# Keys, values and transposed context of the first block, made between the scores of its first unit

## The chip, the cores and the metric

The kernel runs on one core of a Trainium2 chip. Its time is the device time of one execution in microseconds (us). The figure for the kernel before is the median of three runs. Everything else about it comes from one further execution under the hardware profiler.

## The reference, cut to what matters

Four cross-attention layers follow each other on one sequence x of 2048 rows by 256; all read one context of 1601 rows by 512. Layers 0, 2 and 3 are of this form, with 16 heads of 64 (inner width 1024):

```python
q = hidden_states @ Wq                      # 256 -> 1024
k = encoder_hidden_states @ Wk              # 512 -> 1024
v = encoder_hidden_states @ Wv
logits = jnp.einsum('bhqd,bhkd->bhqk', q, k) * HEAD_DIM ** (-0.5)
col_bias = col_bias.at[:, token_indices_A].set((-SUPPRESS * suppress_A_in)[:, None])
col_bias = col_bias.at[:, token_indices_B].set((-SUPPRESS * suppress_B_in)[:, None])
probs = jax.nn.softmax(logits + col_bias, axis=-1)
out = jnp.einsum('bhqk,bhkd->bhqd', probs, v)
out = out @ Wo + bo + residual
```

Two of the 1601 keys for each of A and B (which ones is an input) get a bias that depends on the query row through a mask of 2048 values. Layer 1 has an RMS norm ahead of it, 16 query heads of 16 and 4 key heads, and no bias. All is in float32.

## The kernel before, in words

**Tiles and units.** Keys are cut into 13 chunks (`TCH`, NT = 13): twelve of 128 rows and one of 65. Queries are cut into NB = 4 parts of 512 rows (`QB`). A masked layer has 8 blocks of two heads. A block has four units, one for each query part. A unit runs over the 13 chunks; a step is one chunk of one unit, so a block is 52 steps, and the main loop (L1093) takes steps in pairs. The unit's scores of step s are taken by `masked_scores` (L669): two heads' matmuls into one PSUM pair tile, a copy into a tile of `probs` by ScalarE (L687) and a running maximum by VectorE (L690, L692). When all 13 are done, `maxima` (L728) transposes the maximum on TensorE (L735), reduces it (L736), and sends it through DRAM on to all partitions (L643, L646). The exponentials of the same unit run NT+5 = 18 steps behind its scores: `maxima_spread` (L751) copies the spread maximum into PSUM, `subtract` (L756) is VectorE, `masked_exp` (L761) is ScalarE, and GpSimd adds up the sums (L764, L766). The product with the values (`values`, L801) runs 20 steps behind. So in the steady state TensorE has, for each chunk, scores of one unit and values of an earlier one.

**Pieces.** Work that is not part of a step is kept as pieces with a cost: a unit's queries (L451), denominators (L822), projection (L850), and the keys and values of the next block. `start_block(i)` (L965) loads block i+1's weights and makes its pieces: seven of keys (two chunks of context each, L427) and seven of values (L381). Each takes a context slice that `context_slice` (L245) reads back from DRAM, three slices ahead, into a tile of `work` (`ct`, three buffers). Keys go into `pieces.fill` and values into `pieces.later`, which is released when the last unit of the block before has its values done (L1045), inside the current block; in block 0 that does not happen. A pair of steps takes its due pieces, and, when it scores and exponentiates (`together`, L1130), about one piece of `fill`. At a block's first step `pieces.flush()` (L1032) runs whatever is left.

**The opening.** Before the loop, in this order: the loads of x on ScalarE's DMA queue (L135 to L139); token numbers on SyncE's (`token_numbers`, L147); `key_order` (L164), VectorE arithmetic that puts the biased keys at the end of the context, so that the bias falls into the last chunk: it finds, for each of 13 columns of positions and each of 65 tail positions, the row it comes from (`src`, L223 to L236, 78 columns by 12 tokens); then `first_x` (L574), which transposes x on TensorE, and the first unit's queries. Then L897 to L902 make all keys and values of block 0: `first_context_slice` (L253) gathers the rows of the context by indirect DMA on GpSimd's queue (L260), transposes them on TensorE (L266), copies them out of PSUM, half by ScalarE and half by VectorE, and stores them to DRAM as `ctxT` (L274). Only then does the loop begin. At the third pair of steps `token_rows` (L298) loads the two masks (L301, L302), works them into bias rows (three bfloat16 parts, transposes at L325), and makes `tail_keys` for each masked layer (L332 to L344).

**What sets the order.** L1145 to L1151 tie TensorE, ScalarE and VectorE to the order in which the code writes their instructions. SyncE and GpSimd, with their DMAs, are ordered by the framework's scheduler. Keys, values, queries and bias transposes share one PSUM tile (`pm`, one buffer); score tiles have two buffers (`s`), and a third tile of the same size (`b`) holds the spread maximum. `probs` has 22 buffers. Matmuls of float32 show as two records each.

Of the kernel before, what the change touches and what calls it, by code (L numbers as in the profile page):

```python
# [10 lines left out]
FP = mybir.dt.float32  # L11
# [23 lines left out]
def tile_cross_attention_stack(ctx: ExitStack, tc: tile.TileContext, t: dict, out: bass.AP):  # L35
# [99 lines left out]
    x_rows = [probs.tile([P, QT, C], FP, name="p") for _ in range(NB)]  # L135
    for b in range(NB):
        nc.scalar.dma_start(
            out=x_rows[b], in_=x[0, ts(b, QB), :].rearrange("(n p) c -> p n c", p=P)
        )  # L139
# [7 lines left out]
    def token_numbers():  # L147

        idx = const.tile([P, NTOK], I32, name="tok_idx")
        for l, name in enumerate(masked_names):  # L150
            for s, which in ((0, "A"), (2, "B")):
                nc.sync.dma_start(
                    out=idx[:, 4 * l + s : 4 * l + s + 2],
                    in_=t[name + "token_indices_" + which]
                    .rearrange("(o s) -> o s", o=1).to_broadcast((P, 2)),
                )
# [7 lines left out]
    def key_order(tok):  # L164
# [50 lines left out]
        wide = [P, N, NTOK]  # L215

        def tokens_of(v):
            return v.rearrange("p (o j) -> p o j", o=1).to_broadcast(wide)

        def at_positions(v):  # L220
            return v.rearrange("p (n o) -> p n o", o=1).to_broadcast(wide)

        test = probs.tile(wide, FP, name="p")  # L223
        src = const.tile([P, N], FP, name="src")
        spec = probs.tile([P, N], FP, name="p")
        place = probs.tile([P, N], FP, name="p")
        nc.vector.tensor_tensor(test, at_positions(pos), tokens_of(where), ALU.is_ge)
        nc.vector.tensor_reduce(src, test, AX.X, ALU.add)
        nc.vector.tensor_tensor(src, src, pos, ALU.add)

        nc.vector.tensor_scalar(place, pos, count, float(T), ALU.add, ALU.subtract)
        nc.vector.scalar_tensor_tensor(src, place, 0.0, src, ALU.is_lt, ALU.mult)
        nc.vector.tensor_tensor(test, at_positions(place), tokens_of(rank), ALU.is_equal)
        nc.vector.tensor_tensor(test, test, tokens_of(mine), ALU.mult)
        nc.vector.tensor_reduce(spec, test, AX.X, ALU.add)
        nc.vector.tensor_tensor(src, src, spec, ALU.add)  # L236
        rows = const.tile([P, NT], I32, name="src_rows")
        nc.vector.tensor_copy(rows, src[:, :NT])
        return rows, src[:, NT:]
# [13 lines left out]
    def first_context_slice(i):  # L253

        tiles = [probs.tile([P, 2, 512], FP, name="p") for _ in range(NCT // 2)]
        a0, n0 = TBK[i]
        for c in range(4 * i, min(4 * i + 4, NT)):
            a, n = TCH[c]
            rows = probs.tile([P, CT], FP, name="p")
            nc.gpsimd.indirect_dma_start(  # L260
                out=rows[:n, :], out_offset=None, in_=cond[0],
                in_offset=bass.IndirectOffsetOnAxis(ap=src_rows[:n, c : c + 1], axis=0),
            )
            pt = psum.pair((NCT, P))
            for k in range(NCT):
                nc.tensor.transpose(pt[:, k, :n], rows[:n, ts(k, P)], ident[:n, :n])  # L266
            for k, ct in zip(range(0, NCT, 2), tiles):
                to = ct[:, :, a - a0 : a - a0 + n]
                if k:
                    nc.vector.tensor_copy(to, pt[:, k : k + 2, :n])  # L270
                else:
                    nc.scalar.copy(to, pt[:, k : k + 2, :n])
        for k, ct in zip(range(0, NCT, 2), tiles):
            nc.sync.dma_start(out=ctxT_dram[:, k : k + 2, a0 : a0 + n0], in_=ct[:, :, :n0])  # L274
        return lambda c, k: tiles[k // 2][
            :, k % 2, TCH[c][0] - a0 : TCH[c][0] - a0 + width(c)
        ]
# [20 lines left out]
    def token_rows():  # L298
# [4 lines left out]
        nc.vector.tensor_scalar(masks, masks, -1.0, 1.0, ALU.mult, ALU.add)  # L303
        nc.vector.tensor_scalar(masks, masks, -SUPPRESS, None, ALU.mult)
        bias_cols = probs.tile([P, QT, P], FP, name="p")
        nc.gpsimd.memset(bias_cols, 0.0)
        parts = probs.tile([P, 6, NQ], FP, name="p")
        for m in range(2):
            three_parts(masks[:, m, :], [NQ], lambda i: parts[:, 3 * m + i, :])

        row_of = small.tile([P, 2], FP, name="row_of", bufs=1)
        for j, (r0, r1) in enumerate(((RA, RB), (RB, RE))):
            for h in HALVES:
                nc.vector.tensor_reduce(
                    row_of[h : h + 64, j : j + 1], ident[h : h + 64, h + r0 : h + r1], AX.X, ALU.add
                )
        for b in range(NB):
            for h in HALVES:
                nc.vector.tensor_copy(
                    bias_cols[:, :, h + RA : h + RE],  # L320
                    parts[:, :, b * QT : (b + 1) * QT].rearrange("p r q -> p q r"),
                )
# [4 lines left out]
        for l in range(NL):  # L327


            marks = probs.tile([P, 2, NTAIL], FP, name="p")  # L330
            for to, j in ((0, 0), (1, 2)):
                nc.vector.tensor_scalar(  # L332
                    marks[:, to, :], src_tail, tok[:, 4 * l + j : 4 * l + j + 1], None,
                    ALU.is_equal,
                )
                nc.vector.scalar_tensor_tensor(
                    marks[:, to, :], src_tail, tok[:, 4 * l + j + 1 : 4 * l + j + 2],
                    marks[:, to, :], ALU.is_equal, ALU.max,
                )
            only = probs.tile([P, NTAIL], FP, name="p")  # L340
            nc.vector.tensor_tensor(only, marks[:, 0, :], marks[:, 1, :], ALU.is_gt)

            nc.vector.tensor_scalar(tail_keys[l], only, row_of[:, 0:1], None, ALU.mult)
            nc.vector.scalar_tensor_tensor(  # L344
                tail_keys[l], marks[:, 1, :], row_of[:, 1:2], tail_keys[l], ALU.mult, ALU.add
            )

    bo_of = []
    with nc.allow_non_contiguous_dma(reason="columns of 256 values"):
        for name in masked_names:  # L350
            bo_of.append(const.tile([P, NC], FP, name="bo_" + name))
            nc.gpsimd.dma_start(out=bo_of[-1], in_=t[name + "bo"].rearrange("(k p) -> p k", p=P))
    normw = const.tile([P, NC], FP, name="normw")
    with nc.allow_non_contiguous_dma(reason="one column of 256 values"):
        nc.gpsimd.dma_start(out=normw, in_=t["L1_xattn_norm_w"].rearrange("(k p) -> p k", p=P))

    QUARTERS = (0, 32, 64, 96)  # L360
    den_rows = const.tile([P, 4], FP, name="den_rows")
    one_row = const.tile([P, 1], FP, name="one_row")
    sel = const.tile([64, 4, 4, 32], FP, name="sel")
    nc.gpsimd.memset(sel, 0.0)
# [820 lines left out]
```

## Time and profile before

| What | us |
|---|---|
| median of three runs | 4948.83 (4944.98 to 4951.98) |
| the profiled execution, its own time | 4952.0 |
| its span, first to last instruction | 4950.3 |
| TensorE busy, of the span | 4747.6 (96%) |
| VectorE busy | 3752.7 (76%) |
| first scores of the first unit | 69.42 |
| first scores of block 1 | 243.63 |

The busy shares are of the whole span; the change is in its first 250 us, so windows and the timeline of that stretch say more. Lines of the timeline give the start, the duration, the engine, the line of code and the operation, output first, and in brackets how long the engine was idle and what ended that. Lines of windows give, for each stretch, TensorE's busy time, its weight loads, VectorE, ScalarE and GpSimd, each with a count of instructions, and then the granted TensorE clock, the DMA engines' busy share and GB/s. "PE" is TensorE, "DVE" VectorE, "ACT" ScalarE, "POOL" GpSimd, and "SP" SyncE.

### The profile page before, as it was taken

What the parts mean: (1) busy time and instruction counts of PE and PEld (TensorE: products, weight loads), DVE (VectorE), ACT (ScalarE), POOL (GpSimd) and SP (SyncE); (2) the same over time, 40 slices, a digit from 0 to 9 for tenths busy, and PEclk for the clock granted to TensorE, in tenths of its full rate; (3) what the DMA queues carried; (4) which work ended last, traced back from release to release, by engine and by line L of the source; (5) the groups of instructions that cost most, each with busy time, mean ns of one, the idle gap of its engine ahead of it and who ended that gap; (6) DMA issues with size and microseconds to landing.
All of it is one profiled execution on the core that took longest, in us unless ns stands there. A gap on an engine that the chain in (4) does not pass through costs nothing.

```text
span 4950.3 us, 64060 instructions
## 1 busy us (share of the span) xinstructions
PE 4747.6 (96%) x24004; PEld 2061.6 (42%) x24004; DVE 3752.7 (76%) x3782; ACT 3218.1 (65%) x4000; POOL 2988.8 (60%) x1429
## 2 busy tenths in 40 slices
PE   6899999999999999999999999999999999999996
PEld 4344444444444444444344444444444444444432
DVE  3788888888765666554378888888888888888886
ACT  2677777777634555444467777777777777777774
POOL 1677777777720000000177777777777777777787
PEclk9999999999989999999799999999999999999998
DMA  4222222222201000012133232232222322223211
GB/s 140 65 79 81 80 83 82 81 85 75 71 26 37 19 19 19 26 29 59 29 91 87 77 86 79 82 88 77 78 85 84 84 82 78 79 83 86 78 29 34
DMA packets 352534, 337.88 MB, mean 68 GB/s; under 512 B 120697, under 2 KB 306297, under 8 KB 352224
## 3 DMA queue, kind: packets, MB, share of 16 engines
q1 hardware_dynamic: 348960, 328.41, 23.5%
q8 instruction: 189, 3.10, 0.3%
q0 software_dynamic: 1152, 3.28, 0.2%
q10 hardware_dynamic: 2112, 2.10, 0.1%
q14 instruction: 121, 0.99, 0.1%
HBM read 318.89 MB, written 14.82 MB: 67 GB/s over the span
## 4 chain that ended last, share of the span: by engine, by line
PE 85%; DVE 10%; issue 1%; POOL 1%; ACT 1%; DMA 1%; SPq 0%; POOLq 0%; DVEq 0%; ACTq 0%
PE po L801 27%; PE s L675 19%; PE t L706 8%; PE pm L381 6%; PE pm L427 6%; PE s L850 4%; PE pm L451 4%; PE t L771 3%; DVE rden L826 2%; DVE ntop L736 2%; PE s L822 2%; DVE xs L862 2%; PE s L735 2%; DVE top L692 1%; DVE p L756 1%
## 5 line engine op out<-in xcount | busy, mean ns | idle before, releaser
L766 POOL TENSOR_TENSOR sums<-sums,p 128x1024 f32<-128x1024 f32 (+1 forms) x1152 | 2726.6, 2367 | 754.0 <-ACT p L761 582.2
L687 ACT COPY p<-s 128x1024 f32<-128x1024 f32 (+1 forms) x1248 | 1235.0, 1014 | 680.5 <-PE s L675 590.5
L801 PE MATMUL po<-p,v 128*64 128x512 f32 (+3 forms) x8320 | 1512.2, 531 | 10.4 <-ACT p L761 6.7
L756 DVE TENSOR_TENSOR p<-p,b 128x1024 f32<-128x1024 f32 (+1 forms) x1248 | 1460.9, 1209 | 56.1 <-ACT b L751 54.9
L692 DVE TENSOR_TENSOR top<-s,top 128x1024 f32<-128x1024 f32 (+1 forms) x1056 | 1290.6, 1222 | 233.0 <-ACT p L687 169.6
L675 PE MATMUL s<-q,kT 64*128 64x512 f32 (+1 forms) x4992 | 1348.5, 634 | 91.8 <-DVE ntop L736 23.7
L761 ACT ACTIVATE p<-p 128x1024 f32<-128x1024 f32 (+1 forms) x1248 | 1254.9, 1057 | 51.7 <-DVE p L756 50.3
L801 PEld LDWEIGHTS po<-p,v 128*64 128x64 f32 (+3 forms) x8320 | 368.0, 126 | 1106.3 <-issue 865.3
L675 PEld LDWEIGHTS s<-q,kT 64*128 64x128 f32 (+1 forms) x4992 | 390.6, 182 | 741.8 <-issue 210.2
L783 ACT ACTIVATE p<-t 128x512 f32<-128x512 f32 (+1 forms) x760 | 412.3, 594 | 414.8 <-PE t L706 377.5
L719 DVE TENSOR_REDUCE row_top<-t 128x1 f32<-128x512 f32 x700 | 451.0, 686 | 260.4 <-PE t L706 257.7
L842 POOL TENSOR_TENSOR oT<-oT,by 128x512 f32<-128x512 f32 x112 | 142.9, 1275 | 764.5 <-DMA by<-cols 423.6
L706 PE MATMUL t<-kT,q 32*128 32x512 f32 (+1 forms) x1880 | 562.6, 642 | 0.0
L771 PE MATMUL t<-q,kT 32*128 32x512 f32 (+1 forms) x1520 | 493.7, 662 | 0.0
L706 PEld LDWEIGHTS t<-kT,q 32*128 32x128 f32 x1880 | 294.9, 316 | 168.8 <-issue 84.3
L381 PEld LDWEIGHTS pm<-wv,ct 128*128 128x128 f32 (+1 forms) x2496 | 290.2, 188 | 130.7 <-issue 71.2
L381 PE MATMUL pm<-wv,ct 128*128 128x128 f32 (+2 forms) x2496 | 322.5, 282 | 6.9 <-ACT v L385 3.2
L427 PE MATMUL pm<-ct,wk 128*128 128x256 f32 (+1 forms) x1288 | 301.1, 377 | 0.6 <-DMA wk<-in_L_xattn_Wk_dram 0.6
L736 DVE TENSOR_REDUCE ntop<-s 128x8 f32<-128x1024 f32 x96 | 117.5, 1224 | 229.0 <-PE s L735 229.0
L427 PEld LDWEIGHTS pm<-ct,wk 128*128 128x128 f32 x1288 | 221.0, 190 | 150.0 <-issue 93.6
L764 POOL COPY sums<-p 128x1024 f32<-128x1024 f32 x96 | 99.5, 1036 | 203.2 <-ACT p L761 203.2
L850 PE MATMUL s<-oT,wo 128*128 128x512 f32 x392 | 199.6, 632 | 17.5 <-POOL oT L842 13.6
(155 smaller groups left out, 2356.2 us busy)
## 6 DMA issues: line engine op xcount, KB each, us to landing
ct<-ctxT SPq DMA_DIRECT2D x288, 512.0 KB
xT<-xT SPq DMA_DIRECT2D x100, 512.0 KB
spread<-cols SPq DMA_DIRECT2D x96, 512.0 KB
by<-cols SPq DMA_DIRECT2D x192, 128.0 KB
xT<-xs SPq DMA_DIRECT2D x16, 512.0 KB
ct<-ctxT SPq DMA_DIRECT2D x48, 130.0 KB
wk<-in_L_xattn_Wk_dram SPq DMA_DIRECT2D x24, 256.0 KB
wv<-in_L_xattn_Wv_dram SPq DMA_DIRECT2D x24, 256.0 KB
```

The costliest lines, as they stand in the source:

```text
L381: nc.tensor.matmul(pv[:md, d, :f], ct(k)[:, d * P : d * P + md], wv[:, k, :], start=(k == 0), stop=(k == NCT - 1),)
L427: nc.tensor.matmul(pk, u.wk[:, k, :], ct(k), start=(k == 0), stop=(k == NCT - 1))
L675: nc.tensor.matmul(s[:m, h, :], self.u.kT[r, a : a + m], self.q[r, :], start=True, stop=(a != TAIL),)
L687: nc.scalar.copy(p[:m], s[:m])
L692: nc.vector.tensor_tensor(self.top[:m], s[:m], self.top[:m], ALU.max)
L706: nc.tensor.matmul(s[:, at : at + n], self.q[r, columns(q)], self.u.kT[r, a : a + n], start=True, stop=True,)
L719: nc.vector.tensor_reduce(self.top[:, of, q, k : k + 1], s, AX.X, ALU.max)
L756: nc.vector.tensor_tensor(self.p[c][:m], self.p[c][:m], self.less[:m], ALU.add)
L761: nc.scalar.activation(p[:m], p[:m], AF.Exp)
L766: nc.gpsimd.tensor_tensor(self.sums[:m], self.sums[:m], p[:m], ALU.add)
L771: nc.tensor.matmul(s[:m], self.u.kT[r, a : a + m], self.q[r, :], start=True, stop=True)
L801: nc.tensor.matmul(to, v, p, start=(c == 0 and not part), stop=(c == NT - 1 and part != 0))
```

## The change

- Token numbers are loaded first: A's on SyncE's queue, B's on ScalarE's, and x behind them on ScalarE's queue. The masks are loaded next on SyncE's.
- `key_order` works out the 13 columns of row numbers first, and the gathers (`gather`, two chunks into one tile) are issued at once, all seven. The 65 tail positions follow later (`tail_sources`), after x is transposed.
- `first_x` copies with one ScalarE instruction instead of two halves.
- `first_context_slice` takes two chunks into the `b` tile and one ScalarE copy, into a `ct` tile, and stores it. Keys, context and values of block 0 are made by `first_block(i)`, once in each of the first seven pairs of steps: keys of the next pair of chunks, the slice after that, values of the current pair.
- Mask parts are made before the loop; the columns of the bias are copied by GpSimd; the transposes are four pieces, due at steps 4, 6, 8 and 10. Token marks are made at pair 3 for layer 0 and at pair 7 for the others. Small constants (`bo`, `normw`, `sel`) are loaded and made at pair 7.
- `start_block(0)` is called at pair 7 instead of step 0, and for block 0 values too go into `pieces.fill`. `together` also holds while no unit exponentiates yet.

```diff
@@ before the loop
     made = {(0, 0): layers[0].load(0)}
-    src_rows, src_tail = key_order(tok)
+    x_rows = [probs.tile([P, QT, C], FP, name="p") for _ in range(NB)]
+    for b in range(NB):
+        nc.scalar.dma_start(
+            out=x_rows[b], in_=x[0, ts(b, QB), :].rearrange("(n p) c -> p n c", p=P)
+        )
+    mask_parts, make_mask_parts = masks_parts()
+    src_rows, src_tail, tail_sources = key_order(tok)
+    context_rows = deque(gather(c) for c in range(0, NT, 2))
...
     for b in range(NB):
         first_x(b)
-        keep(0, b)
         if b == 0:
             for _, piece in layers[0].query_pieces(unit_of(0)):
                 piece.run()
-    keys, values = layers[0].projections(made[0, 0])
-    for i in range(NK):
-        ct = first_context_slice(i)
-        for c in range(4 * i, min(4 * i + 4, NT), 2):
-            keys(c, lambda k: ct(c, k))
-            values(c, lambda k: ct(c, k))
-    layers[0].load_wo(made[0, 0])
+    tail_sources()
+    make_mask_parts()
+    biases = [bias_rows_of(b) for b in range(NB)]
...
+    first_keys, first_values = layers[0].projections(made[0, 0])
+    slices = {}
+
+    def first_context(i):
+        c = 2 * i
+        if c < NT:
+            slices[c] = first_context_slice(c, context_rows.popleft())
+
+    def first_block(i):
+        if 2 * i + 2 < NT:
+            first_keys(2 * i + 2, slices[2 * i + 2])
+        first_context(i + 2)
+        if 0 <= 2 * i < NT:
+            first_values(2 * i, slices[2 * i])
+
+    first_context(0)
+    first_block(-1)
+
+    def first_unit(i):
+
+        if i < NT / 2:
+            first_block(i)
+        if i == 1:
+            layers[0].load_wo(made[0, 0])
+            for b in range(NB):
+                keep(0, b)
+                pieces.at(2 * i + 2 + 2 * b, [(0, biases[b])])
+        if i == 3:
+            token_marks(0)
+        if i == 7:
+            small_constants()
+            for l in range(1, NL):
+                token_marks(l)
+            start_block(0)
@@ context
+    def gather(c):
+
+        rows = probs.tile([P, 2, CT], FP, name="p")
+        for d, (_, m) in enumerate(TCH[c : c + 2]):
             nc.gpsimd.indirect_dma_start(
-                out=rows[:n, :], out_offset=None, in_=cond[0],
-                in_offset=bass.IndirectOffsetOnAxis(ap=src_rows[:n, c : c + 1], axis=0),
+                out=rows[:m, d, :], out_offset=None, in_=cond[0],
+                in_offset=bass.IndirectOffsetOnAxis(ap=src_rows[:m, c + d : c + d + 1], axis=0),
             )
-            pt = psum.pair((NCT, P))
...
+        return rows
+
+    def first_context_slice(c, rows):
+
+        ct = work.tile([P, NCT, 2 * P], FP, name="ct", bufs=3)
+        pt = psum.b().rearrange("p d (k j) -> p d k j", j=P)
+        chunks = TCH[c : c + 2]
+        for d, (_, m) in enumerate(chunks):
             for k in range(NCT):
-                nc.tensor.transpose(pt[:, k, :n], rows[:n, ts(k, P)], ident[:n, :n])
...
+                nc.tensor.transpose(pt[:, d, k, :m], rows[:m, d, ts(k, P)], ident[:m, :m])
+        a, n, m = TCH[c][0], width(c), chunks[0][1]
+        nc.scalar.copy(
+            ct[:, :, :n].rearrange("p k (d j) -> p d k j", j=m), pt[:, : len(chunks), :, :m]
+        )
+        nc.sync.dma_start(out=ctxT_dram[:, :, a : a + n], in_=ct[:, :, :n])
+        return lambda k: ct[:, k, :n]
@@ the parts of the masks
+    def bias_rows_of(b):
+
         bias_cols = probs.tile([P, QT, P], FP, name="p")
         nc.gpsimd.memset(bias_cols, 0.0)
...
+        for h in HALVES:
+            nc.gpsimd.tensor_copy(
+                bias_cols[:, :, h + RA : h + RE],
+                mask_parts[:, :, b * QT : (b + 1) * QT].rearrange("p r q -> p q r"),
+            )
+
+        def transposed():
             pt = ps_m.tile([P, QT, P], FP, name="pm")
             for q in range(QT):
                 nc.tensor.transpose(pt[:, q, :], bias_cols[:, q, :], ident)
             nc.vector.tensor_copy(bias_rows[:, ts(b, QB)], pt.rearrange("p a b -> p (a b)"))
...
+        return Piece(transposed, 0.5)
@@ the loop
         (pieces.later if grouped else pieces.fill).extend(first)
-        pieces.later.extend(second)
+        (pieces.later if i else pieces.fill).extend(second)
...
             if place == 0:
                 pieces.flush()
-                start_block(i)
+                if i:
+                    start_block(i)
...
-        if first == 4:
-            token_rows()
...
+        first_unit(first // 2)
-        together = masked(pair[0].scoring) and masked(pair[1].exping)
+        together = masked(pair[0].scoring) and (masked(pair[1].exping) or not pair[1].exping)
```

## The prediction

> **What bounds the kernel now.** I read the page's busy shares first, then the 4-us windows of the opening, the chain of work that ended last, and the timeline. The shares:
>
> ```profile
> PE 4747.6 (96%) x24004; PEld 2061.6 (42%) x24004; DVE 3752.7 (76%) x3782; ACT 3218.1 (65%) x4000; POOL 2988.8 (60%) x1429
> ...
> PE   6899999999999999999999999999999999999996
> ```
>
> PE bounds the whole; only its first two slices (0 to 248 us) and the last fall short, and the first two hold the change. A later block repeats exactly. The negated maximum of unit 0 (L736) comes round in blocks 1 and 2 at:
>
> ```profile
> 285.49 1.22 DVE L736 TENSOR_REDUCE ntop<-s 128x8 f32<-128x1024 f32 x1 [3.29 <-PE s L735]
> ...
> 441.15 1.22 DVE L736 TENSOR_REDUCE ntop<-s 128x8 f32<-128x1024 f32 x1 [3.29 <-PE s L735]
> ```
>
> So a block costs 155.66 us, and the question is how soon the kernel gets into that rhythm. The windows of the opening (PE busy is the second number, PEclk and DMA share near the end):
>
> ```profile
> 16.00:20.00 4.00, 0.14 (x1) 0.00 (x0) 3.86 (x10) 0.00 (x0) 0.00 (x0) 1.00 0.09 29
> 20.00:24.00 4.00, 0.09 (x1) 0.09 (x1) 3.72 (x6) 0.00 (x0) 0.45 (x1) 1.00 0.00 0
> ...
> 80.00:84.00 4.00, 0.00 (x0) 0.00 (x0) 2.63 (x19) 0.00 (x0) 0.00 (x0) 0.89 0.55 134
> 84.00:88.00 4.00, 2.18 (x8) 1.43 (x8) 1.41 (x8) 0.00 (x0) 0.00 (x0) 0.50 0.00 0
> ...
> 232.00:236.00 4.00, 1.31 (x12) 1.11 (x10) 0.00 (x0) 0.37 (x1) 0.00 (x0) 1.00 0.98 326
> ```
>
> Three holes: PE waits for DVE's key order until 24; it waits for masks at 78 to 84, then runs at half clock; it runs dry in the burst of values ahead of block 1. The chain says what each waits for:
>
> ```profile
> 4.04 8.30 DMA tok_idx<-ttn_token_indices_B_dram
> ...
> 75.27 5.61 DMA p<-in_mask_S_fk_dram
> ...
> 229.33 6.81 DMA ct<-ctxT
> ```
>
> The timeline gives three marks: first scores, step 14 (after unit 0's maxima), step 52 (block 1 begins).
>
> ```profile
> 69.42 1.99 PE L675 MATMUL s<-q,kT 64*128 64x512 f32 x8
> ...
> 118.55 1.13 PE L675 MATMUL s<-q,kT 64*128 64x512 f32 x4
> ...
> 243.63 1.99 PE L675 MATMUL s<-q,kT 64*128 64x512 f32 x8
> ```
>
> From step 52 on, the diff touches nothing. The forecast is the new time of that mark.
>
> [...] clock 0.50 at 84 to 88, after idling from 77.9 to 84.7, and two chunks' scores take 3.79 us at 92.1 against 1.99 at 69.42. [...] 4096 values of 4 bytes, 6.2 us from the first issue (74.66) to landing (80.9). [...] what helps the tokens is that x is issued after them.
>
> **Part 1: the start, up to the first scores.** Removed: the tokens' landing at 12.34 behind x (2.1 MB), and the wide part of the key order. Now x follows. Token issues on SP and ACT run in parallel, three each at 0.46 us, until 2.2. A small DMA, cols, takes 3.0 us (119.91 to 122.91), so the last, issued at 1.75, lands near 4.8. The token arithmetic is unchanged: 12.46 to 16.39, 3.9 us. The source arithmetic shrinks from 78 positions by 12 tokens to 13 by 12. No row has 156 elements; 144-element ones (L194 to L203) take 0.31, so five at 0.31, five at 0.17 and the gaps make 2.7 us instead of 6.8. Bounds: 2.4 without gaps, 4 with one of 0.17 each. Row numbers are ready at 11.4 (before 23.3). Gathers take 0.95+0.30 on POOL each, so the first two are issued by 14.0 and, at the median landing of 7.3, are there at 21.3.
>
> The x side decides. ACT was held by its x issues until 12.13, then loaded a table (1.28). Three token issues ahead add 1.4: 13.5, 14.8 after the table. Then x0's single copy (128x1024, as L687, 1.0) to 15.8; queries 2.0 to 17.8; three x transposes at 1.5 (24 records take 4.40) to 22.3; context slice 0's transposes 1.1 and copy 1.0 to 24.4; keys 1.95 and copy 0.4 to 26.8, with slice 1's transposes beneath. The masks are moved up on SP, to where x and weights load: they cost 0 if x is in already, 6.2 if they push it back in full; I take 2.5. First scores: **29.3** instead of 69.42.
>
> What also moves: the x keeps (four SP DMAs) go behind pair 1 and the stores of context become seven; 5.3 MB over some 50 us, where the old opening moved 369 GB/s at 30 to 40. Nothing waits for them until block 1. The bo and norm loads leave POOL's front, four issues (1.40 to 4.90), and are wanted in a layer's last block or by layer 1. Tail sources and mask parts stay on DVE: 5.7 (780 of 936 elements of the old 6.8) and 2.8, done near 22; they cost nothing under the x transposes, since DVE's next work, the first maximum, comes at 31. That is the added wait: if the masks land after 26, unit 0's maxima queue behind it, and PE stops after two score tiles. The eight bias copies go from DVE (0.26 each) to POOL; no POOL row has this shape, its 64x64 copies take 0.19 and 128x1024 takes 1.04, so 1.5 to 8.3 us, on an engine idle from the last gather (28) to the first exponential.
>
> **Part 2: unit 0 (steps 0 to 13).** Each pair of steps now holds on PE two chunks' scores (1.92), next keys (1.95), transposes (1.1), values (2.05): 7.0 us. ACT has 2.0+0.4+1.0+0.4 = 3.8, DVE two maxima at 1.22. The one pm bank (bufs=1) passes from keys to values while the transposes run, 1.1 us against the copy's 0.37+0.1, and from values to keys while the scores run. In the old opening both passes were bare: 0.46 us each (38.10 to 38.52). Sum: scores 6x1.92+2.4 = 13.9; keys 5x1.95+1.1 = 10.9; transposes 4x1.1+0.4 = 4.8; values 6x2.05+1.1 = 13.4; four bias pieces 0.6 (four transposes, as half of L266's eight) with 0.46 of pass each, 4.2; query 2.4; the end, 1.5 wait for the last maximum and 1.2, 2.7. Total 52.3, so step 14 at **81.6** instead of 118.55. But the old stretch also held five key pieces of block 1 (9.7 of PE), which now come later.
>
> **Part 3: steps 14 to 51.** All fourteen pieces of block 1 (keys 6x1.95+1.1, values 6x2.05+1.1: 26.1) run here, one a pair, in 19 pairs. PE: scores 38x0.96 = 36.5; values 32x0.935 = 29.9; three queries 5.8; three maxima and two denominators at 1.2, 6.0; one projection 1.95; tail biases 1.1; pieces 26.1: 107.4. By the same prices a steady block is 151.2, and it takes 155.66, so the factor is 1.03: 110.6. The first exponentials add a stall: DVE's subtraction waits for the spread maxima (8.2 us from ntop to L751's end), its maxima queue behind, and PE wants the score tiles back. Before, that cost 2.87 idle at 131.75 and 1.8 by half clock. Now pieces fill some; between 0 and 6, I take 3. The fourteen token-mark operations of the other two masked layers (seven take 1.85, 92.81 to 94.66, so 3.7) fall here on DVE ahead of its first subtraction, while it has two maxima a pair; a reduction before them waits for POOL, idle by then. Step 52 at 81.6+113.6 = **195.2** instead of 243.63. A gain of 48.4 us. DVE in this stretch: 38x1.22+34x1.17+12 = 98 of 114, as tight as in a steady block (140 of 155.66), so PE stays the bound.
>
> The profiled execution took 4952.0 (span 4950.3 and 1.7 around it), 3.2 above the median of the runs. 4952.0-48.4 = 4903.6; from the median 4948.83, **4900.4**.
>
> **Rivals.** (a) The start is late: x, masks, weights and gathers (6.2 MB) share the DMA engines, slices arrive late. Against: slice 0 is due at 21.3 and slices come each 2.5 us, used each 7. For: gathers landed as late as 9.5, and windows of DMA share 1.0. Twelve us: 4912. (b) The pieces lie on top of a DVE-paced block 0: old steps 14 to 51 took 105.2 (118.55 to 223.7) with 3.1 of keys; 23.0 us of pieces on top make 128.2 instead of 113.6: 4915. For: DVE was near full at 150 to 160. Against: steady blocks hold the same pieces. (c) Nothing changes: SP and POOL orders are not written by hand (L1145 orders PE, ACT, DVE), and if bias copies get between the gathers, these wait for mask parts, and the old prologue returns: 4949, no gain. (d) Slower: the passes of pm in unit 0 are bare and long, [...] its clock stays at half. The 47 us of matmuls double (+45), [...] It decides once pauses and clock cost 48 together; the dense 7.0 per pair speaks against.
>
> **Numbers.** Forecast 66%, own range 4890 (no mask collision, no exponential stall, passes hidden, factor 1.00) to 4913 (6.2 of masks, 6 of stall, factor 1.06, unit 0 5% longer). (a) 15%, (b) 9%, (c) 5%, (d) 5%. Range 4888 to 4918, which takes in (a) and (b). Within 0.2% (9.9 us) is about what a measurement of this kernel can't tell from no change: faster 0.90, same 0.05, slower 0.05.
>
> **What would show it.** First scores near 29; row numbers near 11; PE busy above 9 tenths with clock 1.00 from 30 to 80, no hole at 78 to 92; step 14 near 82; no burst before block 1, step 52 near 195; block period still 155.66. Wrong, if first scores come after 40, if unit 0 takes over 60, or if the clock shows 0.50 for long.

## The result and the profile after

Over six runs of each kernel, the changed one takes **4907.03 us** in the median (4898.06 to 4910.53) and the kernel before 4947.5 (4944.98 to 4951.98): a ratio of 0.9915, with an interval of 0.9902 to 0.9928. The gain is 40.5 us, with an interval of 36 to 49. The profiled execution took 4898.06, the fastest of its six, with a span of 4896.4; the profiled one of before, 4952.0, was the slowest of its six. The profiles alone would give 53.9.

The shares on the page of the changed kernel:

```profile
PE 4727.9 (97%) x24004; PEld 2059.7 (42%) x24004; DVE 3746.8 (77%) x3766; ACT 3221.9 (66%) x3994; POOL 2993.3 (61%) x1440
...
PE   8999999999999999999999999999999999999996
```

As many matmuls as before take 20 us less of PE's time, and PE's second slice reads 9 now, as those after it do. The three marks of the forecast, in the changed kernel's timeline (scores are L687 there, the copy into the score tile's row L699):

```profile
32.54 1.23 PE L687 MATMUL s<-q,kT 64*128 64x512 f32 x2 [3.33 <-issue]
...
84.12 1.13 PE L687 MATMUL s<-q,kT 64*128 64x512 f32 x4
...
195.53 1.99 PE L687 MATMUL s<-q,kT 64*128 64x512 f32 x8
```

The first of these lines ends where its view ended; all eight records of that pair take 3.58 us, against 1.99 later, at half clock (PEclk 0.57 at 32 to 36, below). First scores come at 32.5 instead of 69.4, step 14 at 84.1 instead of 118.6, step 52 at 195.5 instead of 243.6. So 48.1 us are won by the start of block 1. The next blocks begin 155.4 and 155.7 us apart, where the kernel before has 155.1 and 155.6. The windows of the opening (columns as in the prediction: PE busy second, then PEld, DVE, ACT, POOL, PEclk, DMA share):

```profile
20.00:24.00 4.00, 1.48 (x12) 1.00 (x10) 2.65 (x17) 1.83 (x3) 2.85 (x4) 1.00 1.01 350
...
28.00:32.00 4.00, 1.21 (x7) 0.92 (x5) 0.00 (x0) 0.00 (x0) 3.39 (x5) 0.88 1.03 415
32.00:36.00 4.00, 3.46 (x8) 1.19 (x8) 0.00 (x0) 2.40 (x3) 2.42 (x11) 0.57 1.04 406
36.00:40.00 4.00, 4.00 (x30) 3.69 (x29) 1.23 (x1) 2.40 (x3) 0.00 (x0) 1.00 0.93 317
...
80.00:84.00 4.00, 3.52 (x24) 2.29 (x20) 1.22 (x1) 2.14 (x4) 0.00 (x0) 1.00 0.05 14
```

The holes at 78 to 92 and ahead of block 1 are gone. One new hole is there, at 28 to 32, where ACT and DVE do nothing at all and PE is busy for 1.21 of 4 us. The chain of waits names what holds the start now:

```profile
1.77 5.93 DMA tok_idx<-ttn_token_indices_A_dram
...
16.45 4.43 DMA p<-in_ctx_dram,src_rows
...
29.21 3.33 issue
```

The last line, "issue", is a wait for which the profile shows no reason.

The best single view is one window that reaches from the first instruction to step 52. Before:

```profile
0.00:243.63 243.63, 185.25 (x836) 95.64 (x837) 137.09 (x193) 108.48 (x141) 98.03 (x73) 0.93 0.34 99
```

After:

```profile
0.00:195.52 195.52, 170.44 (x836) 93.83 (x836) 127.43 (x175) 111.09 (x135) 99.79 (x84) 0.98 0.41 122
```

The same 836 matmul records lie in both. PE is busy for 185.25 us before and 170.44 after, and idle for 58.4 and 25.1. So of the 48.1 us, 33.3 are waits that are gone and 14.8 are matmuls that no longer run at half clock. The clock records agree: windows at half clock add up to 34.1 us before step 52 in the kernel before and to 6.8 in the changed one, and half of the difference is 13.7.

### The profile page after: what moved, and what is told of

Read it like the earlier page. It is cut to its first block, busy times and chain, and to the rows that moved or that the text cites. A ratio compares the mean times of both kernels' runs of the same rounds, so it can differ in the third digit from the quotient of the medians.

```text
span 4896.4 us, 64042 instructions
## 1 busy us (share of the span) xinstructions
PE 4727.9 (97%) x24004; PEld 2059.7 (42%) x24004; DVE 3746.8 (77%) x3766; ACT 3221.9 (66%) x3994; POOL 2993.3 (61%) x1440
## 4 chain that ended last, share of the span: by engine, by line
PE 87%; DVE 10%; issue 1%; POOL 1%; ACT 1%; DMA 0%; POOLq 0%; SPq 0%; DVEq 0%; ACTq 0%
PE po L813 28%; PE s L687 19%; PE t L718 8%; PE pm L394 7%; PE pm L440 6%; PE s L862 4%; PE pm L464 4%; PE t L783 3%; DVE ntop L748 2%; DVE rden L838 2%; PE s L834 2%; DVE xs L874 2%; PE s L747 2%; DVE top L704 1%; POOL sums L778 1%
## 5 line engine op out<-in xcount | busy, mean ns | idle before, releaser
L699 ACT COPY p<-s 128x1024 f32<-128x1024 f32 (+1 forms) x1248 | 1235.4, 1014 | 663.6 <-PE s L687 578.6
L687 PE MATMUL s<-q,kT 64*128 64x512 f32 (+1 forms) x4992 | 1342.2, 631 | 86.7 <-DVE ntop L748 23.7
L687 PEld LDWEIGHTS s<-q,kT 64*128 64x128 f32 (+1 forms) x4992 | 390.0, 182 | 725.6 <-issue 218.7
L394 PEld LDWEIGHTS pm<-wv,ct 128*128 128x128 f32 (+1 forms) x2600 | 300.4, 187 | 130.3 <-issue 66.9
L394 PE MATMUL pm<-wv,ct 128*128 128x128 f32 (+2 forms) x2600 | 333.3, 281 | 2.2 <-ACT v L398 0.9
L440 PE MATMUL pm<-ct,wk 128*128 128x256 f32 (+1 forms) x1344 | 314.6, 377 | 2.7 <-issue 2.7
L862 PE MATMUL s<-oT,wo 128*128 128x512 f32 x392 | 199.1, 631 | 16.2 <-POOL oT L854 12.5
```

The costliest lines, as they stand in the source:

```text
L394: nc.tensor.matmul(pv[:md, d, :f], ct(k)[:, d * P : d * P + md], wv[:, k, :], start=(k == 0), stop=(k == NCT - 1),)
L440: nc.tensor.matmul(pk, u.wk[:, k, :], ct(k), start=(k == 0), stop=(k == NCT - 1))
L687: nc.tensor.matmul(s[:m, h, :], self.u.kT[r, a : a + m], self.q[r, :], start=True, stop=(a != TAIL),)
L699: nc.scalar.copy(p[:m], s[:m])
```

## The experiments

Four kernels ran on one chip (the kernel before: 4953.85 us there), four on a second (4939.67), four on a third (4945.08). Totals are compared through the kernel before on the same chip; inside an opening, the marks are compared.

**The changed kernel again**, no edit.

> The changed kernel once more, unedited. In the first profile of it the mark of block 1 (first scores of step 52) came 48.1 us earlier than before, the layer without a mask (blocks of layer 1) took 6.8 us less by fewer half-clock windows, and yet the median of six runs gained only 40.5. Theory A: the opening gains 48 in every run, and what the median lacks is chance in how often TensorE falls to half clock in layer 1. Then step 52 comes at 195 to 197 again, the profiled time minus that mark varies with the mean granted clock alone, and five more pairs of runs bring a gain between 42 and 49. Theory B: the opening gains only about 40 in a usual run, for instance because the 4.5 us that PE's signal lagged behind the first keys is longer in others. Then step 52 comes at 200 to 204. Also: does ScalarE's copy of the first keys start at about 32.1 again, 4.5 after the recorded end of the matmuls?

Measured: 4910.51 us, ratio 0.9917 (0.9903 to 0.9931); first scores 31.15, step 52 at 194.19. The gain of 43.3 us lies in the first theory's band, and step 52 comes 0.8 before it. ACT's copy of the first keys starts at 30.73, 5.5 us after the recorded end of the keys. The result repeats. This run is the reference for the next three, on the same chip.

**Values of block 1 given out late.** The edit:

```
-        (pieces.later if i else pieces.fill).extend(second)
+        pieces.later.extend(second)
```

> Block 1's seven pieces of values go to the later queue again and run as one burst before block 1; all else as changed. Theory A (PE paces block 0, pieces cost their PE time wherever they run): steps 14 to 51 get shorter by 13.4x1.03 = 13.8 us from 111.4, to about 98, and the burst takes some 18 to 20 as it did before (223.7 to 243.6). Step 52 at 84+98+19 = 201, 6 us later than 195.5; half clock from thin stretches can add up to 5. Total 4907+6 to +11. Rival (DVE paces block 0, so pieces there are free): steps 14 to 51 stay near 108 to 111 and the burst comes on top: step 52 at 211 to 215, +16 to +20.

Measured: 4920.19, which is 9.7 above the reference; step 52 at 209.51. From the first scores on, the marks agree with the reference within 0.4 us to step 30, and at step 50 this kernel is even 5.1 us ahead, because no values lie between. Then the whole lot runs at once ahead of block 1:

```profile
192.00:198.00 6.00, 5.08 (x43) 4.70 (x42) 3.04 (x3) 0.74 (x2) 2.64 (x2) 1.00 0.61 179
198.00:204.00 6.00, 2.89 (x23) 2.54 (x23) 0.00 (x0) 0.74 (x2) 0.00 (x0) 1.00 0.86 263
204.00:210.00 6.00, 5.08 (x40) 4.33 (x40) 0.00 (x0) 1.01 (x3) 0.00 (x0) 1.00 0.41 107
```

From 198 on DVE (the fourth number) does nothing and ACT (the fifth) next to nothing, while PE works or waits for context slices. Between steps 50 and 52 that costs 17.6 us more than in the reference: 12.5 net, plus 2.8 from a later first score. The total's 9.7 is in the first theory's band; the mark, 15.3 later, lies nearer to the rival's. The burst itself takes 18.2 (191.35 to 209.51), within the theory's 18 to 20. What the theory had wrong is the stretch before it: without the values, step 14 to the burst takes 105.4 where the reference needs 111.4 to step 52, so 6.0 less and not 13.8. PE's busy time falls by 11.0 there (107.6 to 96.6), but its waits grow by 5.0 (3.8 to 8.8): nearly half of the values' time on PE had lain where PE would have waited. That one line of the diff carries 9.7 of the 43.3 us that the change gains on this chip.

**The order of the start undone.** x is issued ahead of the tokens (its four loads move up in the code, not shown), and all 78 positions are worked out before the gathers. B's tokens stay on ACT's queue, so now they stand behind x there, which they did not in the kernel before:

```
-        sources(0, NT)
+        sources(0, N)
...
-        return rows, src[:, NT:], lambda: sources(NT, N)
+        return rows, src[:, NT:], lambda: None
```

> x is loaded ahead of the tokens again and the row numbers come out of one wide piece of arithmetic with the tail positions; all else as changed. Theory A (the chain tokens, row numbers, first two gathers sets the start): row numbers at about 23.3 instead of 14.3, so the first slice of context is 9 us later, and first scores come at 41 to 42 instead of 32.5; total +8 to +9.5. Rival (the first scores wait for something else between 22 and 32, such as the crowd on the DMA engines): first scores at 34 to 36, total +2 to +4.

Measured: first scores at 40.02, 8.9 later than in the reference; step 52 at 204.59, 10.4 later; total 4918.49, 8.0 more. The edit does more than it was meant to: B's tokens are issued from 10.50 on and awaited by DVE until 17.35, and row numbers are written at 27.97, not at the theory's 23.3.

```profile
10.50 3.32 ACTq L152 DMA_DIRECT2D tok_idx<-ttn_token_indices_B_dram  x3
...
31.98 1.12 PE L276 MATMUL b<-ident,p 128*128 128x128 f32 x4 [8.08 <-DMA p<-in_ctx_dram,src_rows]
...
39.26 0.37 ACT L446 COPY kT<-pm 128x256 f32<-128x256 f32 x1 [3.81 <-issue]
40.02 1.99 PE L692 MATMUL s<-q,kT 64*128 64x512 f32 x8
```

Row numbers are 13.8 us later than in the reference, first scores only 8.9. The difference is a wait of ACT, "the gap" further down, which the reference has at its first keys and this kernel has not. Beside the third run of the changed kernel, which has no gap either, row numbers are 13.8 later and first scores 14.2. So the first theory's path holds, from tokens over row numbers and gathers to the first scores; the 8.0 are not the price of the old start, since this one is later.

**Keys and values of block 0 all made ahead of unit 0**, as in the kernel before, with all else changed:

```
-    first_context(0)
-    first_block(-1)
+    first_context(0)
+    for i in range(-1, NT // 2 + 1):
+        first_block(i)
...
-        if i < NT / 2:
-            first_block(i)
```

> Keys, context and values of block 0 are all made before the first scores, as in the kernel before but with the new start and the new slices; unit 0 has nothing of them between its scores; all else as changed. Theory A (what interleaving saves is the bare pass of the pm bank, one of two for each pair of chunks, and the time in which the scores alone wait for ScalarE and VectorE): six and a half pairs at 5.6 and then six and a half at 3.5, with four bias pieces and the queries, some 64 us from where unit 0 now takes 51.6; step 52 at 207 to 209, total +11 to +14. Rival 1 (interleaving is most of the gain): total +25 or more. Rival 2 (interleaving is worth nothing, PE has the same sum of work): total within 4.

Measured: first scores at 67.90, step 14 at 100.22, step 52 at 211.67; total 4920.53, 10.0 more. The opening costs 36.8 us more before the first scores and gives 19.3 back in unit 0, which takes 32.3 us here and 51.6 in the reference: 17.5 at step 52. The first theory is the nearest, but its bands are missed: the mark is later than its 207 to 209, the total less than its 11 to 14. Unit 0 by itself is no work for PE alone:

```profile
71.00:75.00 4.00, 2.53 (x10) 0.60 (x8) 2.92 (x3) 2.21 (x4) 0.00 (x0) 1.00 0.32 110
...
83.00:87.00 4.00, 2.17 (x12) 0.83 (x11) 3.75 (x9) 1.24 (x2) 0.00 (x0) 1.00 0.00 0
87.00:91.00 4.00, 2.24 (x12) 0.72 (x8) 3.55 (x4) 2.02 (x2) 0.00 (x0) 1.00 0.01 2
```

PE is busy for 2.2 to 2.5 of 4 us; DVE's maxima and the bias copies set the pace. That idle time of PE is what the making of block 0 is put into.

**Masks late in the changed kernel**: the mask loads, and DVE's mask parts behind them, go back behind the second pair of unit 0 (a fill of the mask tile by DVE holds the loads there).

```
-    make_mask_parts()
-    biases = [bias_rows_of(b) for b in range(NB)]
...
         if i == 1:
+            make_mask_parts()
+            biases = [bias_rows_of(b) for b in range(NB)]
```

> The changed kernel, with the two mask loads and the mask parts moved back behind the first pairs of unit 0, about where the kernel before had them. Theory A (the old hole of 17.4 us between the scores at 74.66 and those at 92.1 was dear because PE had nothing else there: now keys, values and transposes lie in it, and the bias transposes stay pieces): from first scores to step 14 takes 57 to 61 us instead of 51.6, so 5 to 9 more, no long stretch at half clock; the median 4915 to 4920 beside 4910.5 of the repeated changed kernel. Rival (PE works in order, so scores that wait for a maximum hold all that is behind them): 66 to 69 us, 14 to 18 more, with half clock again; 4924 to 4929.

Measured: unit 0 takes 49.97 us, no longer than without the edit on a chip whose opening is otherwise alike (49.98, below); total 4895.7, ratio 0.9903 (0.988 to 0.9925), step 52 at 188.56. Both expectations are missed: the cost is nothing. The comparison of unit 0 is between two chips, one profile each; the last run of this section has the masks late beside the unedited kernel on one chip, with the same answer. The timeline of this kernel shows why:

```profile
38.98 1.37 SPq L306 DMA_DIRECT2D p<-in_mask_S_fk_dram  x1
...
42.11 1.99 PE L441 MATMUL pm<-ct,wk 128*128 128x256 f32 x8
43.41 0.18 DVE L307 TENSOR_SCALAR p<-p 128x32 f32<-128x32 f32 x1 [4.90 <-DMA p<-in_mask_S_fk_dram]
...
45.99 2.55 DVE L705 TENSOR_TENSOR top<-s,top 128x1024 f32<-128x1024 f32 x2
...
47.88 1.99 PE L688 MATMUL s<-q,kT 64*128 64x512 f32 x8
```

DVE waits 4.90 us for the masks and, with the parts behind them, is 7.5 us away from its maxima (38.5 to 45.99). But a pair of unit 0 now lasts 6.5 to 7.7 us on PE, of which DVE needs 2.5. The chain that left a hole of 17.4 us in the kernel before lies in DVE's own idle time.

**Stores of x issued late, from ACT's queue:**

```
-                keep(0, b)
+                nc.scalar.dma_start(out=xT_dram[0][b], in_=xs[:, b])
```

> The changed kernel, with the four stores of the transposed x issued from ACT's queue in the second pair, where the program has them, instead of from SP's, which ran them at 16 to 27 us beside the gathers. Theory A (the 4.5 to 8 us between the recorded end of the first keys and ACT's copy of them, and the late landings, come from these 2.1 MB that SP issues early): the copy follows the keys within 0.3 us, first scores at 25 to 28 instead of 31.2 to 34.0, step 52 at 189 to 192, if ACT has room for the issues. Rival 1 (the gathers alone fill the DMA engines, the stores have no part in the lag): first scores at 31 to 34 as before, step 52 at 194 to 197. Rival 2 (four issues at 0.5 to 0.9 on ACT, in order, hold the copies of keys and scores): unit 0 is 2 to 4 us longer than 51.6.

Measured: first scores at 25.71, ACT's copy 0.1 us after the keys, step 52 at 188.61; total 4890.11, ratio 0.9903 (0.9886 to 0.992). Unit 0 takes 51.5, since the four issues hold ACT by 1.5 in pairs 2 and 3. By itself this looks like the first theory. It isn't: the unedited kernel, further down, has no gap on another chip either.

**The mask part alone, put into the kernel before.** Masks loaded early, parts made at the end of the opening, bias columns on POOL, bias transposes as pieces, token marks in later pairs:

```
-        if first == 4:
-            token_rows()
...
+        if i == 1:
+            for b in range(NB):
+                pieces.at(2 * i + 2 + 2 * b, [(0, biases[b])])
```

> The kernel before, with the mask part of the change alone: masks loaded behind the first weights, their parts made by DVE at the end of the opening's list, bias columns by POOL, the four bias transposes as pieces of unit 0's later pairs, token marks in later pairs. Theory A (the hole from 74.66 to 92.1 with the half clock after it costs 14.7 us against the pattern without it): first scores still near 69.4, step 14 at 104 to 107 instead of 118.55, and about as much earlier at step 52; median 11 to 15 under the kernel before. Rival (part of it comes back: DVE holds unit 0 anyway, and block 1's five key pieces that ran there move to the burst before block 1): step 14 at 104 to 110, but step 52 earlier by 4 to 7 only.

Measured: 4946.34 us, ratio 1.0009 (1.0003 to 1.0016), no gain at all. At step 6 it is 18.0 us ahead of the kernel before, at step 14 only 5.5 (113.02, later than both expectations), and step 52 comes at 234.07. How the hole came back, in the later repetition of this kernel:

```profile
83.43 0.66 PE L326 MATMUL pm<-ident,p 128*128 128x128 f32 x4
...
87.42 0.29 DVE L356 SCALAR_TENSOR_TENSOR tail_keys<-p,row_of,tail_keys 128x65 bf16<-128x65 f32 x1
87.63 0.68 DVE L327 CAST bias_rows<-pm 128x512 bf16<-128x512 f32 x1
88.37 3.17 PE L442 MATMUL pm<-ct,wk 128*128 128x256 f32 x8 [4.28 <-DVE bias_rows L327]
...
97.36 1.99 PE L442 MATMUL pm<-ct,wk 128*128 128x256 f32 x8 [2.85 <-DVE bias_rows L327]
```

A bias piece writes the one pm bank; DVE copies it out only behind two maxima (2.55) and the seven token marks (1.85); the next keys wait for the bank, and PE's scores wait behind the keys. Three such waits, of 4.28, 2.85 and, ahead of a query, 2.89, take back most of the hole.

**The token part alone, put into the kernel before** (tokens ahead of x on two queues, the 65 tail positions while DVE waits for the masks):

> The kernel before, with the token part of the change alone: tokens ahead of x, split over SP's and ACT's queues, the wide part of the key order for the 65 tail positions made later, while DVE waits for the masks. Theory A (the opening was held by DVE's key order until 24 us and everything behind it moves up): row numbers at 14 instead of 23.1, first scores at 60 to 62 instead of 69.42, the same 8 to 9 at step 52 and in the median. Rival (gathers, stores of x and of context share the DMA engines at 1.0, so that the opening is held by them and gives most of it back): first scores at 65 to 68, 2 to 4 in the median.

Measured: row numbers at 14.2 and first scores at 60.25, 9.2 us earlier, as the first theory has it. By step 2 it is 9.6; then the hole at the masks grows by 3.3, since DVE makes the tail positions there (69.0 to 74.8) and the masks are in before it is done, and 6.3 stay. Step 52 comes at 235.98, 7.7 before the kernel before's first profile and 2.1 before its second, which follows. The ratio is 0.9991 (0.9982 to 0.9999), about 4.5 us.

**The kernel before again**, no edit, now with a profile.

> The kernel before once more, with a profile of its own beside the other kernels of the same chip. Theory A (its opening repeats, and runs differ only by how many windows of half clock fall into the later layers): first scores within 1 us of 69.42, step 52 within 2 of 243.63, and the total follows the half-clock time after step 52, half a microsecond for each. Rival (the opening itself differs from run to run): step 52 off by more than 5 us.

Measured: 4944.91, first scores at 69.81, step 14 at 118.23, but step 52 at **238.09**, 5.5 us earlier than in the profile that the forecast was made from. The work is the same. Windows at half clock before step 52 add up to 20.5 us here and to 34.1 there. The rival is right for this one stretch, steps 14 to 51.

**The changed kernel a third time**, no edit.

> The changed kernel a third time, to have it on the same chip as the two others. Theory A (stores of x from SP and masks together delay the start): the gap between the end of the first keys and their copy is there a third time, first scores at 31 to 34, step 52 at 194 to 197, ratio to the kernel before 0.990 to 0.993. Rival (the gap is chance): first scores below 28.

Measured: 4899.75, ratio 0.9909 (0.9894 to 0.9923); first scores at **25.83**, step 52 at **187.20**. The first theory falls. In the profile of the result, ACT's copies of the first slice and of the first keys stand like this:

```profile
23.60 1.01 ACT L273 COPY ct<-b 128x1024 f32<-128x1024 f32 x1 [2.17 <-remote]
...
32.11 0.37 ACT L441 COPY kT<-pm 128x256 f32<-128x256 f32 x1 [7.50 <-remote]
```

Here, with the same program:

```profile
21.96 1.01 ACT L273 COPY ct<-b 128x1024 f32<-128x1024 f32 x1 [0.41 <-PE b L271]
...
25.06 0.37 ACT L441 COPY kT<-pm 128x256 f32<-128x256 f32 x1 [2.08 <-PE pm L440]
```

PE's records put the end of those keys at 27.6 there and at 25.0 here, and the end of the slice's transposes at 21.9 in both. So the copy of the slice is 1.7 late there and that of the keys 4.5, and with 1.0 more for the keys themselves that accounts for the 6.7 us between the first scores of the two. ("remote" stands where the profile names no instruction as the releaser.) Neither the masks nor the stores of x make this gap by themselves: both are as early here. It is in the result's profile and in three kernels of the first chip (the changed one again, values late, block 0 ahead), and in none of the eight kernels on the second and third.

**The mask part alone, once more.**

> The kernel before with the mask part alone, once more: in the first try step 52 came 9.6 us earlier than in the profile of the kernel before, yet the median was 0.1% above that of the kernel before. Theory A (its later layers happened to get more windows of half clock on that chip, a matter of chance): on this chip the ratio is 0.997 to 0.999, that is 5 to 15 us faster. Theory B (the half clock that is taken out of the opening comes back in the later layers): ratio 0.9995 to 1.002 again, with step 52 still 8 to 11 us earlier and more half-clock time after it than in the kernel before.

Measured: ratio 0.9986 (0.9976 to 0.9995), some 7 us less than the kernel before; the medians are 4941.26 and 4945.08. Step 14 comes 5.1 us earlier than in the kernel before on this chip, step 52 5.4 (232.66 against 238.09). So the mask part alone wins about 5 us in the opening, and the total is 7 us less on this chip and 4 us more on the other. The ratio here is theory A's, the one on the other chip was theory B's; the two intervals don't meet, and no run says why.

**Masks and stores of x both late** in the changed kernel (one store a pair, from ACT).

> The changed kernel with both put behind the start: masks as in the late-masks run, and the four stores of x from ACT's queue, one a pair in pairs 1 to 4. Theory A (either of the two is enough to clear the start, and late masks cost nothing in unit 0): first scores at 25.5 to 27.5, step 52 at 186 to 189, 6 to 8 us less than the changed kernel beside it. Rival (the two add up: with both gone gathers land earlier still): first scores below 24.5 and step 52 below 186. Other rival (late masks and stores meet in unit 0 and hold it): step 52 at 190 to 194.

Measured: first scores at 25.03, step 52 at 187.22; total 4899.26, ratio 0.9906 (0.9892 to 0.9921). The unedited kernel beside it has 187.20 and 4899.75. Nothing is won: neither was on the path there. No version tried here is shown to be faster than the change.

## Why the prediction came out as it did

The forecast, 4900.4, is 6.6 us under the median. Its main mark, step 52 at 195.2, was measured at 195.5. Both agreements are in part luck, since errors cancel, so here is each step; the third column is the third run of the changed kernel, without the gap.

| step | forecast | result's profile | third run |
|---|---|---|---|
| tokens landed | 4.8 | 7.7 | 7.7 |
| row numbers | 11.4 | 14.2 | 14.2 |
| second gather landed | 21.3 | 20.9 | 21.2 |
| x copy, queries, their end | 15.8, 2.0, 17.8 | 12.6, 3.8, 16.5 | 13.2, 3.8, 17.0 |
| first scores | 29.3 | 32.5 | 25.8 |
| unit 0 | 52.3 | 51.6 | 50.0 |
| steps 14 to 51 | 113.6 | 111.4 | 111.4 |
| step 52 | 195.2 | 195.5 | 187.2 |

**The start.** Tokens took 5.93 us from issue to landing, not 3.0: the row of another small DMA (119.91 to 122.91), from a quiet stretch (DMA share 0.05), was no measure for one that is in flight beside x (0.36 from 1.77 to 7.70). The same load took 8.30 behind x in the kernel before, and at most 4.0 where its last issue, at 13.36, came after x's own (the start undone). The error of some 2.9 went on into the row numbers. It was cancelled by the gathers: the median landing of 7.3 came from a stretch with the DMA share at 0.90 to 1.04 (28 to 40 in the kernel before), and the second one took 4.43 after its issue, though the share was 1.10 there (16.45 to 20.88); what made it shorter is not shown. ACT was free of its issues at 10.3 instead of 13.5, as x's four issues took 8.09 us and not the 11.28 of the kernel before. The queries took 3.78 and not 2.0: I had taken the price of a later stretch, while the kernel before shows half of its first queries at 2.08 in the same place. That is what half clock would cost, but no clock record covers it: they begin at 18.7 us in the result's profile. The 2.5 us for the masks fail: they landed at 20.2, with x and the gathers in time. "The x side decides" fails too, narrowly: x's transposes ended at 20.4, PE waited 0.46 for the second gather, and the chain of waits runs through tokens, row numbers and gathers. The forecast without the masks' term is 26.8, and the runs without the gap have 25.0 to 27.2.

**The gap**, 1.7 and 4.5 us at two copies, and the half clock after it, is what no step of mine contained. A slow start had been my rival (a), with late slices as its cause; slices were there (PE waited 0.46 for the second gather). The cause stays open. The profiles of the first chip and of the result also lack semaphore records, most of them of DMA landings and some of PE, between about 16 and 32 us in those with the gap: their traces hold 32,951 to 32,958, and 33,055 with the start undone, where the four late kernels of the other two chips (the changed one a third time, masks late, stores late, both late) hold 33,174 to 33,178. So lost records and the gap go together; which is cause and which effect, no run separates.

**Unit 0.** 52.3 against 51.6 and 50.0. Pairs without a bias piece took 6.50 (forecast 7.0), pairs with one 7.68. The passes of the pm bank lie under other work, as said. The late-masks run shows what the forecast had not asked: DVE has some 4 us to spare in a pair (2.55 of 6.50 for two maxima).

**Steps 14 to 51.** The sum of PE work was 107.4; the window from step 14 to step 52 shows 107.6 busy, in the result's profile and in the third run alike. The waits are 3.8, where I had 6.2 (a factor of 1.03 and 3 for the first exponentials). This is the best step of the forecast. But the run with the values late shows that a sum of PE work alone doesn't hold here: taking 11.0 of it out shortened the stretch by 6.0 only.

**From step 52 on** the gain was to be carried to the end. In profiles it is, apart from the clock: in fourteen profiles, span less step 52 less half of the half-clock time after step 52 is 4601.6 to 4609.4 us, whatever the kernel. That half-clock time lies between 182 and 218 us and moves a total by up to 17. In the clock records of the two profiles that the forecast and the result come from, every half-clock stretch but the last of each has a length of 3.413 us or a multiple (32 stretches and 27). The same program, the kernel before, had 34.1 and 20.5 us of half clock in its opening in two runs; why the two differ, no run shows.

**Where 8 us of the gain went.** Forecast 48.4, profile 48.1, median 40.5. The step of the forecast that failed, as far as these runs show, is its base: "4952.0-48.4" took one execution's opening, half clock and all, as the kernel's. The second profile of the kernel before has step 52 at 238.09 instead of 243.63; from there, the gain at step 52 is 42.6 for the result's profile and 50.9 for the third run, on the chip of that 238.09. Which of the two openings is the usual one, two profiles can't say. Totals also differ by less than marks: 9.7 against 15.3 (values late), 8.0 against 10.4 (start undone) and 10.0 against 17.5 (block 0 ahead), each beside the changed kernel, and 45.3 against 50.9 for the third run beside the kernel before. More half clock in the later layers could be the reason, but it isn't shown. An estimate from the runs' mean clocks, given in thousandths, less the half clock of the openings, finds 10 to 15 us more of it after step 52 in the five runs that keep the whole change than in the kernel before, if that kernel's opening is put at the mean of its two profiles; it finds 3 to 8 with 20.5 for that opening and 17 to 22 with 34.1, and for the kernel before, run again, it finds 5 more than for that same kernel. In the profiles, the third run has 193.5 us after step 52, both late 210.8, the kernel before of that chip 196.0; in the first pair it is 182.9 against 199.7.

**The rivals.** (b), pieces on top of a DVE-paced block: 128.2 forecast, 111.4 measured; gone. (c), nothing changes: the gathers did keep their place on POOL, which also put the bo and norm loads and the small constants ahead of them (1.4 to 7.4 us), at no cost. (d), half clock throughout: the clock was at 1.00 from 35.8 us to the end of the opening.

**Not a sum of parts.** In the opening, the mask part alone is worth 4 to 11 us and the token part alone 2 to 8, by which profile of the kernel before is taken. Taken out of the changed kernel, the interleaving costs 17.5 at step 52 (10.0 in the total), the early values 15.3 (9.7), the start, put back later than it was, 10.4 (8.0), and the early masks nothing. The old hole at the masks was closed by the work that lies beside it, not by loading the masks sooner.

## What to carry to other kernels

A wait on a transfer need not be removed if the engine that bounds the kernel can be given work to lie beside it: the same mask chain cost a hole of 17.4 us alone and nothing between keys and values. Removing a hole by itself may win little, because the next shared buffer (here one PSUM bank, copied out by a busy DVE) made a new one. Work that was put into waits cost less than its own time: the values kept PE busy for 11.0 us and lengthened their stretch by 6.0. And before a forecast of some 10 us is made from one profile, the half-clock windows in it should be counted: the same kernel had 34.1 us of them in one opening and 20.5 in another.

## What the hardware showed that I had not expected

- The same program, in two runs, had ACT's copy of the first keys 0.1 us and 4.5 us after the end of the matmuls that it waits for, with first scores at 25.8 and 32.5. It came in a stretch (28 to 32) of DMA share 1.03 and 415 GB/s; but the run with the masks late, which is without it, had 1.02 to 1.06 and 406 to 411 GB/s there.
- 4096 mask values of 4 bytes took 9.4 us from the first issue (10.80) to landing (20.2) beside x and the gathers, at no cost to the start; in unit 0 they took 4.9 (38.53 to 43.41).
- 836 matmul records took 185.25, 170.44 and, in the third run with no half clock after its records begin, 166.45 us of PE:

```profile
0.00:187.20 187.20, 166.45 (x836) 91.33 (x836) 127.73 (x175) 110.83 (x135) 99.75 (x84) 1.00 0.43 127
```
